# An attention and mixture-of-experts kernel: elementwise work on shared weights and on the residual moved between GpSimd and VectorE

## The chip, the core and the metric

The kernel runs on one core of a Trainium2 chip. The core has five engines that run their own instruction streams and meet at semaphores: TensorE (PE, matrix products; PEld is its weight load), VectorE (DVE), ScalarE (ACT), GpSimd (POOL) and SyncE (SP, which here only issues DMAs). The metric is the device time of one execution in microseconds (us). The kernel before takes 664.94 us, the median of 6 runs that lie between 659.42 and 669.69 us.

## The reference

Four sequences of 512 tokens with 256 features go through two residual blocks.

```python
# block 1: an expert chosen per sequence, then attention with 16 heads that share one key and value
expert = argmax(cond_8, -1)
hidden = silu(x @ W_up[expert].T + b_up) * (x @ W_gate[expert].T + b_gate)
c = hidden @ W_down[expert].T + b_down
q = (c @ Wq.T + bq) / 4 ;  k, v = split(c @ Wkv.T + bkv)
x = x + softmax(q @ k.T) @ v @ Wo.T + bo
# block 2: a linear map mixed per sequence, then a routed feed-forward net, 2 of 8 experts
masked_w = weight * mask[None]                     # weight is [8, 256, 256]
w_bot = einsum('bg,got->bot', cond_8, masked_w)    # one mixed 256x256 weight per sequence
z = x @ w_bot.T + bias
x = x + ffn(z)                                     # router, capacity 128, gelu, combine
```

Three elementwise parts of this matter here: `weight * mask` (8 tiles of 128x512 numbers), the sum over the 8 masked weights for each sequence (8 multiply-adds of 128x512 per sequence), and the addition of `bo` to the residual `x` of each sequence (4 tiles of 128x256).

## The kernel before, in words

**Phases.** The first expert net and the projections of sequence 0 run alone (up to about 43 us). Then comes one long loop over steps n = -8 to 64, of 4 quarters i each, that does the attention of all four sequences (to about 388 us); its gaps are filled with the other matrix work. Then 18 routed units of the feed-forward net run one after the other on PE (to about 606 us), and a tail writes the last rows.

**A step.** The loop stands at lines 1370 to 1393. In each quarter it issues `maxima` for the step 8 ahead (one matmul at L444 into one of 3 buffers `pm`, then a DVE maximum at L446), `exponentials` (a matmul at L473 into one of 2 buffers `pe`, then an ACT exponential at L474), whatever is pending, and then, in the third quarter of every even step, `weigh` (L483: 16 matmuls of two finished steps with the values). Such a quarter is said to weigh; it issues no further matrix work. After that come the pieces that were put at this step and quarter with `at(n, i, ...)`. In the other quarters `pump` takes pieces of side work from `tracks`, each a list of pieces with a start step and an end step, the one furthest behind first. From step 38 on, a quarter in `shut` issues a `fill` in place of `pump`: one matmul on zeros (L499).

**Engine order.** Each engine works through its instructions in exactly the order of these calls. An instruction that waits holds back everything behind it on its engine, and nothing else.

**The parts that the change touches.** The masks are multiplied on GpSimd while the loads of `w2` are issued (L249 to L252). `mixing(b, g)` (L567) adds one masked weight to the mixed weight `wb`; for sequences 0 and 1 it is two GpSimd instructions (L582, L583; L579 for g = 0), for 2 and 3 one DVE instruction (L577; L575 for g = 0). `residual(b)` (L558) loads `x` into one buffer, `residual_bias(b, n)` (L563) adds `bo` to a quarter of it on GpSimd. `prepared` (L585) is three DVE instructions at step -5: a copy of a 0/1 pattern, `spread`, and two products that make `bias2_b`, which `router_bias` (L592) reads one step later. `routed_weights(b)` (L598) turns `wb` on PE (L606) and multiplies it with the router's weight (L619); it comes after the last `mixing` of its sequence. `finish(b)` (L632) uses `x` in its first four pieces (L650) and `wb` in `mix` (L691). The scatter of finished rows (L839) and the loads of the first routed weights (L1082, L1108) are issued from GpSimd's queue.

Of the kernel before, what the change touches and what calls it, by code (L numbers as in the profile page):

```python
# [9 lines left out]
F32 = mybir.dt.float32  # L10
# [4 lines left out]
ALU = mybir.AluOpType  # L15
# [3 lines left out]
P = 128  # L19
# [3 lines left out]
D = 256  # L23
NE = 8
# [30 lines left out]
def adaln_attn_ffn_kernel(  # L55
# [21 lines left out]
    nc = tc.nc  # L77
# [24 lines left out]
    def side():  # L102
        while len(pending) > (0 if opened or crossed else 1):
            take_out()
        crossed[:] = opened
        return pside.tile([P, 512], F32, tag="side", name="side")
# [39 lines left out]
    seqs = [{} for _ in range(B)]  # L146
# [16 lines left out]
    def load(ap, shape, name):  # L163
        t = const.tile(shape, F32, name=name)
        nc.sync.dma_start(t, ap)
        return t
# [8 lines left out]
    bo_sb = load(bo[0:1, :].to_broadcast([P, D]), [P, D], "bo_sb")  # L175
    bias_x = const.tile([P, DX], F32, name="bias_x")
    nc.sync.dma_start(bias_x[:, 0:D], bias2[0:1, :].to_broadcast([P, D]))
    bias2c_sb = load(bias2c, [P, 2], "bias2c_sb")
# [4 lines left out]
    ones = const.tile([P, P], F32, name="ones")  # L183
# [34 lines left out]
    spread = const.tile([P, P], F32R, name="spread")  # L218
    bias2_b = const.tile([P, 2, P], F32, name="bias2_b")
# [11 lines left out]
    for n in range(2):  # L231
        t = const.tile([P, P], F32, name=f"negm{n}")
        nc.gpsimd.memset(t, 0.0)
        negm.append(t)
    for n in range(B):
        t = const.tile([P, 4, 32], F32, name=f"v{n}")
# [3 lines left out]
    rp = ctx.enter_context(tc.tile_pool(name="rp", bufs=1))  # L240
    attn_ctx = ExitStack()
    apool = attn_ctx.enter_context(tc.tile_pool(name="apool", bufs=1))
    for n in range(4):
        t = apool.tile([P, 4, T], F32R, name=f"qq{n}")
        nc.gpsimd.memset(t[64:65].bitcast(F32), 0.0)
        qq.append(t)
    w2_sb = apool.tile([P, NE, 2 * D], F32, name="w2_sb")
    m2_sb = cp.tile([P, 2 * D], F32, name="m2_sb", bufs=1)
    nc.sync.dma_start(m2_sb, mask2.rearrange("p c o -> p (c o)"))  # L249
    for g in range(NE):  # L250
        nc.sync.dma_start(w2_sb[:, g, :], w2[:, g].rearrange("p c o -> p (c o)"))
        nc.gpsimd.tensor_tensor(w2_sb[:, g, :], w2_sb[:, g, :], m2_sb, ALU.mult)  # L252
    bqs_sb = const.tile([P, 2], F32, name="bqs_sb")

    qp = attn_ctx.enter_context(tc.tile_pool(name="qp", bufs=1))
    ep = attn_ctx.enter_context(tc.tile_pool(name="ep", bufs=2))
# [304 lines left out]
        seqs[b]["x"] = t  # L561

    def residual_bias(b, n):  # L563
        t = seqs[b]["x"][:, n, :]
        nc.gpsimd.tensor_tensor(t, t, bo_sb, ALU.add)  # L565

    def mixing(b, g):  # L567
        if g == 0:
            seqs[b]["wb"] = rp.tile([P, 2, DX], F32, name="wb", bufs=2)
        wb = seqs[b]["wb"][:, :, 0:D]  # L570
        w = w2_sb[:, g, :].rearrange("p (c o) -> p c o", c=2)
        k = cond_sb[:, b * NE + g : b * NE + g + 1]
        if b > 1:
            if g == 0:
                nc.vector.tensor_scalar(wb, w, k, None, ALU.mult)  # L575
            else:
                nc.vector.scalar_tensor_tensor(wb, w, k, wb, ALU.mult, ALU.add)  # L577
        elif g == 0:
            nc.gpsimd.tensor_scalar(wb, w, k, None, ALU.mult)  # L579
        else:  # L580
            t = rp.tile([P, 2, D], F32, name="wk")
            nc.gpsimd.tensor_scalar(t, w, k, None, ALU.mult)  # L582
            nc.gpsimd.tensor_tensor(wb, wb, t, ALU.add)  # L583

    def prepared():  # L585
        nc.vector.tensor_copy(spread, bias2_b[:, 0])
        for c in range(2):
            nc.vector.tensor_scalar(
                bias2_b[:, c, :], ones, bias2c_sb[:, c : c + 1], None, ALU.mult
            )  # L590

    def router_bias():  # L592
        pl = pex.tile([P, T], F32, name="pe")
        for c in range(2):
            mm(pl[:, 0:NE], bias2_b[:, c, :], wr_sb[:, c, :], start=c == 0, stop=c == 1)
        return lambda: nc.scalar.copy(bias_x[:, D:DX], pl[:, 0:NE])

    def routed_weights(b):  # L598

        s = seqs[b]  # L600

        def turned():
            pt = side()
            for oc in range(2):
                for c in range(2):
                    nc.tensor.transpose(  # L606
                        pt[:, ds(oc * D + c * P, P)], s["wb"][:, c, ts(oc, P)], ident
                    )

            def take():  # L610
                s["wbT"] = rp.tile([P, 2, D], F32, name="wbT")
                nc.scalar.copy(s["wbT"].rearrange("p o c -> p (o c)"), pt)
            return take

        def times():
            pl = side()
            for c in range(2):
                for oc in range(2):
                    mm(  # L619
                        pl[:, ts(c, NE)], s["wbT"][:, oc, ts(c, P)], wr_sb[:, oc, :],  # L620
                        start=oc == 0, stop=oc == 1,
                    )

            def take():
                nc.scalar.copy(
                    s["wb"][:, :, D:DX], pl[:, 0 : 2 * NE].rearrange("p (c e) -> p c e", c=2)
                )
            return take

        return [(512, turned), (512, times)]  # L630
# [639 lines left out]
    def defer(take):  # L1270
        if take and take is not OPEN:
            pending.append(take)

    def track(start, end, pieces):
        tracks.append([start, end, sum(c for c, _ in pieces), 0, list(pieces)])
# [33 lines left out]
    track(18, 32, conditioned(3))  # L1309
    track(32, 35, project(3))  # L1310
    for b in range(B):
        track(*((11, 16), (27, 32), (50, 54), (60, 64))[b], routed_weights(b))
    rest = [finish(b) for b in range(B - 1)]
    for b in range(B - 1):
        track(16 * b + 22.75, 16 * b + (28, 28, 24.5)[b], rest[b][:4])
# [6 lines left out]
    def at(n, i, what, *args):  # L1322
        later.setdefault((n, i), []).append((what, args))
# [16 lines left out]
            sides.add((end + 5, 2))  # L1340
    for b in range(B):
        at((14, 30, 45, 58)[b], 0, residual, b)
        for n in range(4):
            at((17, 33, 46, 61)[b] + n // 2, 2 * (n % 2), residual_bias, b, n)
        for g in range(NE):
            n, i = divmod((0, 64, 167, 223)[b] + (4, 4, 4, 2)[b] * g, 4)
            at(n, i, mixing, b, g)
            shut.add((n, i))
    for i in range(9):
        at(4 + 2 * i, 0, clear, i)  # L1350
    units = [("first", n) for n in range(FIRST)] + [("early", n) for n in range(EARLY)]
# [2 lines left out]
        ("last", 1), ("last", 5), ("last", 2), ("last", 3),  # L1354
    ]
    ahead, turned, go, _ = routed(units[:-1])
    at(-5, 0, prepared)
    at(-4, 1, lambda: defer(router_bias()))
    first = list_parts(full_list("first", FIRST))
    for k in range(12):  # L1360
# [170 lines left out]
```

## Time and profile before

One execution was profiled. It took 665.37 us, and its span, first to last instruction, is 663.7 us.

| | busy us | share of the span | instructions |
|---|---|---|---|
| PE | 622.6 | 94% | 2812 |
| DVE | 342.7 | 52% | 916 |
| ACT | 238.0 | 36% | 430 |
| POOL | 173.2 | 26% | 179 |

A busy share is a mean over phases with different limits, and the records of matmuls overlap, so that PE can show as busy and still wait a little. In a table by stretches, a row has the stretch in us from the span's start, its length, the busy time and number of instructions of each engine, then the granted TensorE clock (1.00 is full speed), and what the DMA engines did. In a timeline, a row has the start, the duration, the engine, the line, the operation, the tiles and the number of instructions merged into the row; in square brackets stand the idle time of the engine before it and what ended it. In a row of a group of instructions, "busy, mean" is followed by the engine's idle time just before them.

### The profile page before, as it was taken

How to read it: one execution, taken by the hardware profiler on the slowest of the kernel's cores; microseconds unless marked ns; L12 is line 12 of the kernel's file. 1: busy time of each engine (PE TensorE's matmuls, PEld its weight loads, DVE VectorE, ACT ScalarE, POOL GpSimd, SP SyncE). 2: the span in 40 equal slices, each digit the busy share in tenths (PEclk: the TensorE clock that was granted, in tenths of full speed). 3: DMA queues.
4: the chain of work that ended last, by engine and by line, in shares of the span. 5: the costliest groups of instructions: out<-in, count | busy, mean ns of one | idle time of the engine just before them, and what ended most of it. 6: DMA issues, size and time to landing. Idle time of an engine off the chain costs nothing.

```text
span 663.7 us, 8215 instructions
## 1 busy us (share of the span) xinstructions
PE 622.6 (94%) x2812; PEld 408.4 (62%) x2812; DVE 342.7 (52%) x916; ACT 238.0 (36%) x430; POOL 173.2 (26%) x179
## 2 busy tenths in 40 slices
PE   8989999999999999899997879999999999999992
PEld 3444454454465555555454357888888897878882
DVE  3379866668766568888685441256212221223231
ACT  2231556565555455555454541211211112111110
POOL 7496000049000100042032250106312222021331
PEclk9999999999999999999797898999999999999997
DMA  7673275558321242333023836536765778456221
GB/s 240 225 180 129 91 224 157 173 152 258 114 65 38 82 129 55 97 89 112 24 92 97 315 114 262 156 121 212 227 172 160 236 230 250 149 162 193 61 26 17
DMA packets 53844, 97.64 MB, mean 147 GB/s; under 512 B 8418, under 2 KB 37378, under 8 KB 49154
## 3 DMA queue, kind: packets, MB, share of 16 engines
q1 hardware_dynamic: 46562, 81.98, 38.6%
q0 software_dynamic: 7232, 15.04, 9.6%
q8 instruction: 25, 0.41, 0.2%
q14 instruction: 25, 0.20, 0.1%
HBM read 67.50 MB, written 29.50 MB: 146 GB/s over the span
## 4 chain that ended last, share of the span: by engine, by line
PE 69%; DMA 12%; DVE 6%; POOL 5%; ACT 3%; issue 2%; SPq 1%; another core or an unknown queue 1%; POOLq 0%; DVEq 0%
PE psC L1216 14%; PE psA L1150 12%; PE pa L483 9%; PE pe L473 8%; PE pm L444 8%; DMA out_dram<-y,at 7%; PE side L338 4%; PE side L322 3%; DVE negm L446 2%; PE side L691 2%; PE side L369 2%; PE side L643 2%; ACT e L474 2%; POOL w_sb L252 2%; DMA inv_rows<-invs 2%
## 5 line engine op out<-in xcount | busy, mean ns | idle before, releaser
L446 DVE TENSOR_REDUCE negm<-pm 128x1 f32<-128x512 f32 x256 | 168.0, 684 | 61.7 <-PE pm L444 58.7
L474 ACT ACTIVATE e<-pe 128x512 f32<-128x512 f32 x256 | 148.2, 599 | 137.5 <-PE pe L473 125.6
L444 PE MATMUL pm<-kk,qq 65*128 65x512 f32 x256 | 146.8, 579 | 4.0 <-DVE negm L446 2.5
L1216 PE MATMUL psC<-wo_sb,hT 128*128 128x256 f32 (+2 forms) x544 | 115.2, 381 | 1.0 <-DVE xTr L1127 1.0
L473 PE MATMUL pe<-qq,kk 67*128 67x512 f32 x256 | 109.1, 431 | 6.9 <-ACT e L474 6.4
L1150 PE MATMUL psA<-xTr,wi_sb 128*128 128x256 f32 (+5 forms) x512 | 109.4, 371 | 3.4 <-ACT hT L1154 3.4
L1216 PEld LDWEIGHTS psC<-wo_sb,hT 128*128 128x128 f32 (+2 forms) x544 | 93.2, 182 | 17.2 <-issue 1.7
L1154 ACT ACTIVATE hT<-psA 128x512 f32<-128x512 f32 (+3 forms) x72 | 38.9, 544 | 180.7 <-PE psA L1150 162.5
L1150 PEld LDWEIGHTS psA<-xTr,wi_sb 128*128 128x128 f32 x512 | 92.2, 194 | 17.9 <-ACT hT L1154 3.6
L1196 POOL DMA_INDIRECT out_dram<-y,at x34 | 52.3, 1538 | 186.1 <-DVE w L1176 78.4
L444 PEld LDWEIGHTS pm<-kk,qq 65*128 65x128 f32 x256 | 49.1, 192 | 60.0 <-issue 24.7
L473 PEld LDWEIGHTS pe<-qq,kk 67*128 67x128 f32 x256 | 50.0, 196 | 40.5 <-ACT e L474 28.0
L338 PE MATMUL side<-xT_sb,w 128*128 128x512 f32 x128 | 62.4, 596 | 4.7 <-ACT u L295 2.6
L483 PE MATMUL pa<-e,v 128*32 128x512 f32 x512 | 66.2, 637 | 0.0
L1127 DVE COPY xTr<-psC 128x512 f32<-128x512 f32 (+5 forms) x18 | 10.5, 594 | 82.6 <-PE psC L1123 77.1
L1193 DVE TENSOR_SCALAR y<-psC,w 128x256 f32<-128x256 f32 (+1 forms) x30 | 14.4, 481 | 74.4 <-PE psC L1216 74.4
L565 POOL TENSOR_TENSOR x<-x,bo_sb 128x256 f32<-128x256 f32 x16 | 12.3, 785 | 137.4 <-DMA x<-in_xtok_dram 81.9
L839 POOL DMA_INDIRECT xp<-x,to_i x32 | 32.2, 1007 | 48.4 <-DVE negm L446 27.5
L338 PEld LDWEIGHTS side<-xT_sb,w 128*128 128x128 f32 x128 | 23.7, 190 | 22.0 <-issue 10.3
L483 PEld LDWEIGHTS pa<-e,v 128*32 128x32 f32 x512 | 13.8, 112 | 32.3 <-issue 32.0
L322 PE MATMUL side<-hid,w 128*128 128x512 f32 x64 | 31.6, 595 | 0.4 <-DVE hid L304 0.3
L582 POOL TENSOR_SCALAR wk<-w_sb,cond_sb 128x512 f32<-128x512 f32 x14 | 22.6, 1612 | 1.0
(274 smaller groups left out, 536.8 us busy)
## 6 DMA issues: line engine op xcount, KB each, us to landing
wi_sb<-in_wi_dram SPq DMA_DIRECT2D x14, 1024.0 KB
wo_sb<-in_wo_dram SPq DMA_DIRECT2D x14, 1024.0 KB
xp<-zeros SPq DMA_DIRECT2D x8, 1072.0 KB
qq<-qd SPq DMA_DIRECT2D x32, 256.0 KB
ov<-o SPq DMA_DIRECT2D x16, 256.0 KB
xt<-xp SPq DMA_DIRECT2D x15, 268.0 KB
w<-in_wcond_dram SPq DMA_DIRECT2D x12, 256.0 KB
wi_sb<-in_wi_dram POOLq DMA_DIRECT2D x3, 1024.0 KB
```

The source lines that it names most:

```text
L322: mm(po, wd[:, hc, ts(dc, P)], s["hid"][:, hc, :], start=hc == 0, stop=hc == 3)
L338: mm(s["ps"], s["w"][:, ds(first + P * c, P)], s["xT"][:, c, :], start=c == 0, stop=c == 1,)
L444: mm(pm, qq[u % 4][0:KMAX, hh, ts(i, P)], kk[0:KMAX, :], start=True, stop=True)
L446: nc.vector.tensor_reduce(negm[u % 2][:, c : c + 1], pm, AX.X, ALU.max, negate=True)
L473: mm(pe, kk[0:KEXP, ts(kc, P)], qq[u % 4][0:KEXP, i, :], start=True, stop=True)
L474: nc.scalar.activation(e_of[n][:, i, :], pe, AF.Exp)
L483: mm(pa_of[u][32 * i : 32 * i + 32, :], seqs[u // 4]["v"][:, kc, :], e[:, i], start=False, stop=kc == 3,)
L839: i = nc.gpsimd.indirect_dma_start(out=xp, out_offset=bass.IndirectOffsetOnAxis(ap=to_i[:, k, ch : ch + 1], axis=0), in_=s["x3"][:, ch, :] ...
L1150: mm(ph[:, f, :], wi_of[t][:, c, ts(first + f, P)], xT_of[t][:, c, 0:size], start=c == 0, stop=c == 1,)
L1154: nc.scalar.activation(hT_of[t][:, ds(first, per), 0:size], ph, AF.Gelu_apprx_tanh)
L1196: a = nc.gpsimd.indirect_dma_start(out=out_rows, out_offset=bass.IndirectOffsetOnAxis(ap=at[0:m, i : i + 1], axis=0), in_=y[0:m, i, :], in ...
L1216: mm(po[lo : lo + m, i % 2, :], hT_of[t][:, fc, ds(i * P, m)], wo_of[t][:, fc, :], start=fc == lo // REST, stop=fc >= F // P - (2 if m <= ...
```

## The change

- The 8 mask products go from GpSimd, at the load, to DVE (`masked`), at the third quarter of steps 0, 2, ..., 14. All but the first of these quarters weigh.
- The mixed weights of sequences 0 and 1 go from GpSimd to DVE, in the form that sequences 2 and 3 already had (2 GpSimd instructions become 1 DVE instruction). Sequence 0's stand at the second quarter of the odd steps 3 to 17, sequence 1's at quarters that weigh, steps 18 to 32.
- Sequence 2's mixed weights, on DVE as before, are spread from steps 41 to 48 (one a step) over steps 40 to 51 (one every 6 quarters). Two of the eight stand at quarters that weigh.
- The residual's bias goes from GpSimd (16 instructions of 128x256) to DVE (8 of 128x512), up to 6 steps later than before.
- `prepared` goes from DVE at step -5 to GpSimd, into the set-up part, ahead of the loop.
- The tracks of `routed_weights` for sequences 0, 1 and 2 move to later steps.

```diff
     for g in range(NE):
         nc.sync.dma_start(w2_sb[:, g, :], w2[:, g].rearrange("p c o -> p (c o)"))
-        nc.gpsimd.tensor_tensor(w2_sb[:, g, :], w2_sb[:, g, :], m2_sb, ALU.mult)
     bqs_sb = const.tile([P, 2], F32, name="bqs_sb")
+    nc.gpsimd.tensor_copy(spread, bias2_b[:, 0])
+    for c in range(2):
+        nc.gpsimd.tensor_scalar(
+            bias2_b[:, c, :], ones, bias2c_sb[:, c : c + 1], None, ALU.mult
+        )
...
     def residual_bias(b, n):
-        t = seqs[b]["x"][:, n, :]
-        nc.gpsimd.tensor_tensor(t, t, bo_sb, ALU.add)
+        t = seqs[b]["x"][:, ds(2 * n, 2), :]
+        nc.vector.tensor_tensor(t, t, bo_sb.unsqueeze(1).to_broadcast([P, 2, D]), ALU.add)
+
+    def masked(g):
+        nc.vector.tensor_tensor(w2_sb[:, g, :], w2_sb[:, g, :], m2_sb, ALU.mult)
...
         k = cond_sb[:, b * NE + g : b * NE + g + 1]
-        if b > 1:
-            if g == 0:
-                nc.vector.tensor_scalar(wb, w, k, None, ALU.mult)
-            else:
-                nc.vector.scalar_tensor_tensor(wb, w, k, wb, ALU.mult, ALU.add)
-        elif g == 0:
-            nc.gpsimd.tensor_scalar(wb, w, k, None, ALU.mult)
+        if g == 0:
+            nc.vector.tensor_scalar(wb, w, k, None, ALU.mult)
         else:
-            t = rp.tile([P, 2, D], F32, name="wk")
-            nc.gpsimd.tensor_scalar(t, w, k, None, ALU.mult)
-            nc.gpsimd.tensor_tensor(wb, wb, t, ALU.add)
-
-    def prepared():
-        nc.vector.tensor_copy(spread, bias2_b[:, 0])
-        for c in range(2):
-            nc.vector.tensor_scalar(
-                bias2_b[:, c, :], ones, bias2c_sb[:, c : c + 1], None, ALU.mult
-            )
+            nc.vector.scalar_tensor_tensor(wb, w, k, wb, ALU.mult, ALU.add)
...
-        track(*((11, 16), (27, 32), (50, 54), (60, 64))[b], routed_weights(b))
+        track(*((20, 26), (37, 42), (51.5, 54.5), (60, 64))[b], routed_weights(b))
...
     for b in range(B):
         at((14, 30, 45, 58)[b], 0, residual, b)
-        for n in range(4):
-            at((17, 33, 46, 61)[b] + n // 2, 2 * (n % 2), residual_bias, b, n)
+        for n in range(2):
+            at((19, 35, 51, 61)[b] + (2, 2, 2, 1)[b] * n, 1, residual_bias, b, n)
         for g in range(NE):
-            n, i = divmod((0, 64, 167, 223)[b] + (4, 4, 4, 2)[b] * g, 4)
+            n, i = divmod((13, 74, 162, 223)[b] + (8, 8, 6, 2)[b] * g, 4)
             at(n, i, mixing, b, g)
             shut.add((n, i))
+    for g in range(NE):
+        at(2 * g, 2, masked, g)
...
-    at(-5, 0, prepared)
```

## The prediction

> **What bounds the kernel now.** I read the busy time by stretches first, since the share over the span mixes phases.
>
> ```profile
> core 0: us, PE busy (x) PEld busy (x) DVE busy (x) ACT busy (x) POOL busy (x), PEclk, DMA share, GB/s
> 44.00:72.00 28.00, 26.48 (x80) 14.16 (x79) 26.13 (x45) 5.34 (x9) 16.83 (x12) 1.00 0.50 137
> 72.00:158.00 86.00, 83.50 (x366) 43.82 (x365) 60.61 (x105) 50.89 (x93) 16.15 (x13) 1.00 0.59 177
> 158.00:250.00 92.00, 89.41 (x399) 48.05 (x398) 61.28 (x106) 50.17 (x92) 10.82 (x11) 0.98 0.34 97
> 250.00:315.00 65.00, 61.82 (x311) 34.41 (x310) 55.70 (x134) 36.95 (x68) 11.67 (x14) 1.00 0.30 90
> 315.00:388.00 73.00, 66.50 (x309) 33.97 (x308) 46.62 (x159) 35.88 (x67) 15.79 (x21) 0.84 0.35 123
> ```
>
> PE binds the loop. DVE is its rival only at two places: before step 0 (44 to 72 us: 93% busy) and from 250 to 315 us (86%). From 72 to 250 us, where most of the new DVE work goes, it is 67 to 70% busy. After 388 us nothing is changed. The waits say the same: from 72 to 158 us DVE's maxima wait 18.6 us for PE, and PE waits 0.3 us for DVE.
>
> Next, the timelines, for what GpSimd's work does to DVE:
>
> ```profile
> 25.04 10.70 POOL L252 TENSOR_TENSOR w_sb<-w_sb,m_sb 128x512 f32<-128x512 f32 x8 [11.40 <-DMA w_sb<-in_w_dram]
> ...
> 31.58 1.63 DVE L395 TENSOR_TENSOR qL<-q,qH 128x512 fp32r<-128x512 f32 x1
> 34.05 0.57 DVE L381 CAST qH<-q 128x512 fp32r<-128x512 f32 x1 [0.84 <-ACT q L377]
> 34.66 1.64 DVE L395 TENSOR_TENSOR qL<-q,qH 128x512 fp32r<-128x512 f32 x1
> ...
> 39.44 3.70 PE L338 MATMUL side<-xT_sb,w 128*128 128x512 f32 x8 [0.63 <-ACT u L295]
> 43.34 0.47 PE L444 MATMUL pm<-kk,qq 65*128 65x512 f32 x1 [0.20 <-DMA qq<-qd]
> ```
>
> L395 takes 1.63 us beside the masks and 0.68 us with GpSimd idle (its shortest of 8 is 681 ns). The maxima, which read PSUM, show no such thing: 665 to 694 ns throughout.
>
> ```profile
> 55.38 0.50 DVE L586 CAST spread<-bias_b 128x128 fp32r<-128x128 f32 x1
> ...
> 55.91 1.51 DVE L588 TENSOR_SCALAR bias_b<-ones,bias2c_sb 128x128 f32<-128x128 f32 x2
> ...
> 58.13 0.47 PE L444 MATMUL pm<-kk,qq 65*128 65x512 f32 x1 [1.25 <-POOL wb L583]
> ```
>
> PE's 1.25 us are put down to GpSimd, but L444 doesn't read `wb`. The maxima behind L588 start at 57.35, and PE goes on when the first has emptied a `pm` buffer: the wait is `prepared`'s. The chain of waits names GpSimd before 57 us for the same false reason; I don't count it.
>
> Last, a quarter that weighs, where DVE idles while PE does 1.85 us of L483:
>
> ```profile
> 112.42 1.29 DVE L446 TENSOR_REDUCE negm<-pm 128x1 f32<-128x512 f32 x2 [1.66 <-PE pm L444]
> ```
>
> **The change part by part**, on the profiled execution (665.37 us, 0.43 above the median of the runs).
>
> *Start, -1.1 us.* Without masks on GpSimd each L395 is 0.95 us shorter. The second query waits for the first L395 (ACT idles 2.24 us), so the second L395 ends 2.1 us sooner, and the queries' DMAs and L313 with it. PE takes of this the 0.63 us that it waited for `u` (whose L291 waited 2.44 us for L313), 0.26 us inside the 3.70 (8 such matmuls at 0.43 us are 3.44) and the 0.20 us for `qq`: 1.1 us. Between 0 and -2.1.
>
> *`prepared`, -1.25 us.* DVE loses 0.50 + 1.51 us where it is 93% busy; PE gets its wait back. On GpSimd the three stand after the `qq` memsets (end 13.6 us), need `bias2c` (issued at 16.6 us), and are used at step -4 (59.5 us). Between 0 and -2.0.
>
> *GpSimd's mixing of sequence 1, -0.8 us.* From 142 to 166 us it stretches DVE's L395 (1.18 and 0.94 for 0.68), L381 (0.69 for 0.43), L409 (0.71 for 0.41) and L527 (1.22 for 0.19): 2.35 us. Little reaches PE: L418 waits 0.79 us for `kv`, behind the queries. I take that; between 0 and -2.4.
>
> *Masks, 0.* Nearest row: L395 alone, the same operation and shape, 0.68 us; eight are 5.4 us. Seven stand in quarters that weigh, under 1.66 us of DVE idling. If that cover is gone, 0.68 each: 0 to +5.4. The weights were loaded by 36 us, 36 us before the first mask.
>
> *Sequence 0's mixing, +0.7 us.* 0.48 (L575) + 7 x 0.743 (L577) = 5.7 us at quarters that do not weigh. The same instructions from 250 to 315 us hold 2.2% of that stretch's chain of waits, 1.4 us of their 5.7: 25%, with DVE 86% busy. In 72 to 158 us DVE goes from 60.6 to some 71.7 us, 83%, coming from 70%; I take half of that quarter, 12%. Between 0 and +5.7. Behind each stands the next maximum, and PE can run ahead by three `pm` buffers.
>
> *Sequence 1's mixing, 0.* Another 5.7 us, all in quarters that weigh, one per two steps; at 25% +1.4.
>
> *Residual's bias, +0.8 us.* Eight of 0.68 us (as L395) replace 12.3 us on GpSimd. Two are at steps 35 and 37, where DVE is 84% busy: 25%, 0.35. Six at 12%: 0.5. Between 0 and +5.4. They wait for `x`: if it came late all maxima would queue behind. GpSimd began its adds at 141.3, 221.8, 302.0 and 364.4 us, so `x` was there; the new places (L473 of steps 19, 35, 51, 61) start at 163.8, 249.4, 322.4 and 371.7: 7 us of margin at least.
>
> *Sequence 2's mixing, -0.3 us.* The same eight instructions; two now stand in quarters that weigh: 2 x 0.74 x 25% = 0.4, less a little for the late ones. Between -1.4 and +0.3.
>
> *Moved tracks and GpSimd's queue, 0.* The same PE work per sequence moves inside a loop that PE binds. GpSimd loses 10.7 + 3.8 + 22.6 + 19.3 + 12.3 = 68.7 us, but its scatters wait for DVE's row numbers. No DMA is moved past another on SP.
>
> Sum: -1.1 - 1.25 - 0.8 + 0.7 + 0.8 - 0.3 = -1.95, so 663.4 for an execution like the profiled one, 663.0 as a median.
>
> [...] The granted clock first:
>
> ```profile
> 226.10:229.50 3.40, 3.40 (x19) 2.50 (x18) 2.43 (x4) 2.65 (x6) 0.00 (x0) 1.00 0.00 0
> 229.50:232.90 3.40, 3.40 (x6) 1.68 (x6) 1.44 (x3) 1.40 (x3) 0.00 (x0) 0.50 0.03 5
> ```
>
> PE shows no idle stretch, and yet the next 3.4 us run at half speed: short delays can cost the clock. [...]
>
> Against moving work to DVE: L839, GpSimd's scatter, takes 1.25 us at 346.8 us beside a DVE L577, and 0.97 at its shortest. [...] The scatters run at 289 to 300, 340 to 351 and after 385 us, where hardly any DVE work is new.
>
> **Rivals.** (1) *DVE becomes the bound in steps 3 to 37*: `pm` backs up behind the mixing and the bias, which then cost full length. Against it: 18.6 us of DVE waiting for PE; for it: DVE at 83%, and PE's weight loads for L444 already wait 21.8 us for maxima over the whole run. Gains stay at -3.45; 5.7 + 5.4 = 11.1 on top give 673.0, 672.6 as a median. It decides once PE waits over 5 us for DVE from 72 to 250 us. (2) *GpSimd's contention was worth its full length*: lower bounds -2.1 - 2.0 - 2.4 - 1.4 = -7.9 with nothing paid: 657.5, 657.0 as a median. For it: DVE and PE are both full from 44 to 72 us, so each us saved may count on both. Against it: PE's own waits there are 1.5 us. (3) *The clock*: two more 6.8 us windows at half speed, +6.8 at most, 669.8; two fewer, 656.2. (4) *The change doesn't do what it says*: sequence 0's mixing stands in no quarter that weighs; that is in the sum.
>
> **How the numbers follow.** Forecast 0.57, rival 1 0.14, rival 2 0.19, rival 3 0.10 split evenly. The single runs before spread by 10 us, and a change of under 1% (6.6 us) is about what can't be told from none. Rival 2, half of rival 3 and a forecast that misses low give 0.25 below 658.3; rival 1, the other half and one that misses high give 0.18 above 671.6; 0.57 between. The range, 655 to 673, reaches to rival 2 with a shorter clock loss below and to rival 1 above; some 2 in 10 lie outside.
>
> **What would show it.** Right: L395 at 0.7 us near 32 us, first L444 near 42.2 us, no 1.25 us wait near 57 us, DVE near 78 to 83% from 72 to 158 us with PE still waiting under 2 us for it, L527 at 0.2 us throughout. Wrong: `negm` on the chain of waits from 72 to 250 us beyond 5%, a DVE wait for `x`, or half-speed windows before 229 us.

## The result and the profile after

The changed kernel takes 669.78 us (median; 664.44 to 676.53), the kernel before 665.47 us in all its runs beside it. The ratio is 1.0074, 95% interval 1.0058 to 1.009: the change makes the kernel slower by about 4.9 us by this ratio (by 4.3 us between the two medians). The forecast was 663.0 us, 1.95 us less than before: the sign is wrong, though the time lies inside the wide range. Ratios, and the half-speed times below, leave out the runs that took over 1.5% longer than the fastest of their kernel. The profiled execution took 669.92 us, its span is 668.2 us, its mean granted clock 0.969, as before.

The busy time by the same stretches, after:

```profile
core 0: us, PE busy (x) PEld busy (x) DVE busy (x) ACT busy (x) POOL busy (x), PEclk, DMA share, GB/s
44.00:72.00 28.00, 27.73 (x87) 15.46 (x85) 25.92 (x44) 7.42 (x13) 0.00 (x0) 1.00 0.49 143
72.00:158.00 86.00, 82.99 (x365) 42.14 (x364) 69.17 (x122) 50.22 (x92) 0.00 (x0) 1.00 0.62 180
158.00:250.00 92.00, 88.11 (x396) 48.32 (x396) 67.22 (x119) 51.13 (x93) 0.00 (x0) 1.00 0.30 89
250.00:315.00 65.00, 61.33 (x308) 33.59 (x307) 51.62 (x125) 34.60 (x66) 8.66 (x10) 0.97 0.29 86
315.00:388.00 73.00, 65.43 (x296) 31.52 (x299) 45.79 (x153) 34.85 (x66) 10.74 (x16) 0.84 0.36 123
```

GpSimd is empty from 44 to 250 us, and DVE is 80% busy from 72 to 158 us, as forecast. The last two rows hold fewer instructions of PE and DVE than before: work is late there. The same engines' timelines at the start (DVE, then PE) show the gain:

```profile
31.54 0.69 DVE L399 TENSOR_TENSOR qL<-q,qH 128x512 fp32r<-128x512 f32 x1
33.06 0.43 DVE L385 CAST qH<-q 128x512 fp32r<-128x512 f32 x1 [0.84 <-ACT q L381]
33.53 0.69 DVE L399 TENSOR_TENSOR qL<-q,qH 128x512 fp32r<-128x512 f32 x1
...
56.66 1.37 DVE L450 TENSOR_REDUCE negm<-pm 128x1 f32<-128x512 f32 x2 [0.40 <-PE pm L448]
```

```profile
41.67 0.68 PE L448 MATMUL pm<-kk,qq 65*128 65x512 f32 x1
```

L399 (L395 before) takes 0.69 us in place of 1.63, the first maximum's matmul starts at 41.67 in place of 43.34 us, and without `prepared` between the maxima near 57 us PE's wait of 1.25 us is gone. How this gain is kept and lost is read by comparing the start of the same step (its first `pe` matmul, L473 before, L477 after) in the two traces:

| step | 0 | 14 | 16 | 36 | 42 | 46 | 50 | 54 | 56 | 58 | 62 |
|---|---|---|---|---|---|---|---|---|---|---|---|
| before, us | 71.8 | 137.6 | 147.9 | 252.5 | 278.4 | 296.9 | 314.5 | 335.3 | 344.3 | 359.6 | 374.7 |
| after less before, us | -3.1 | -3.0 | -3.9 | -4.7 | -1.3 | +1.0 | -0.2 | +4.7 | +8.1 | +3.6 | +3.6 |

The changed kernel is 4.7 us ahead at step 36. It loses this and more at steps 36 to 46 and 50 to 56. (The 4.5 us that it regains between 56 and 58 are a pause in the trace of before: ACT idles 4.7 us near 350 us, and no record says for what. Such a pause of 4.7 to 5.2 us, with 3.4 or 6.8 us at half speed behind it, is in five of the twelve traces of kernels whose second half of sequence 2's router stands at its old place, and in none of the eight where it is moved. One trace of a kernel can't tell how often its runs have it.)

What happens near step 53 shows the kind of loss. PE's timeline before, and after:

```profile
333.15 0.20 PE L782 MATMUL side<-hot,upto_b 128*128 128x64 bf16 x1
333.19 0.19 PE L786 MATMUL side<-prev,ones_b 128*128 128x64 bf16 x1
333.22 0.17 PE L790 MATMUL side<-total,ones_b 128*128 128x16 bf16 x1
333.25 0.47 PE L444 MATMUL pm<-kk,qq 65*128 65x512 f32 x1
333.79 0.50 PE L473 MATMUL pe<-qq,kk 67*128 67x512 f32 x1
334.13 0.40 PE L543 MATMUL side<-inv_rows,spread 128*128 128x512 f32 x1
```

```profile
334.55 0.17 PE L783 MATMUL side<-total,ones_b 128*128 128x16 bf16 x1
335.32 1.03 PE L612 MATMUL side<-wr_sb,wbT 128*128 128x8 f32 x8 [0.60 <-DVE m L459]
336.20 0.47 PE L448 MATMUL pm<-kk,qq 65*128 65x512 f32 x1
336.52 0.39 PE L477 MATMUL pe<-qq,kk 67*128 67x512 f32 x1
337.66 0.79 PE L547 MATMUL side<-inv_rows,spread 128*128 128x512 f32 x1 [0.75 <-ACT wb L618]
```

The second half of sequence 2's router (L612; L619 before) was done at step 52.0 before. Now it stands between the counts (L775 to L783) and L547, and all of them take turns in the `side` banks. PE waits 0.60 us for DVE, does 1.03 us of matmuls with only 8 columns, and waits 0.75 us for ACT's copy. By stretches of 3.4 us, after:

```profile
333.70:337.10 3.40, 2.60 (x17) 1.76 (x16) 2.76 (x7) 1.98 (x5) 0.00 (x0) 1.00 0.23 82
337.10:340.50 3.40, 2.84 (x8) 1.62 (x8) 2.31 (x10) 1.10 (x3) 0.00 (x0) 0.50 0.01 5
340.50:343.90 3.40, 3.40 (x11) 1.50 (x14) 2.97 (x10) 1.79 (x3) 0.00 (x0) 0.50 0.02 5
343.90:347.30 3.40, 3.40 (x17) 0.90 (x10) 0.00 (x0) 0.00 (x0) 2.75 (x3) 0.50 0.23 81
```

Waits of 1.35 us in all, none longer than 0.75, are followed by 10.2 us at half the granted clock (1.00, then 0.50 three times). Other such waits are new: 2.0 us at step 42.25 (L779, whose input L764 stands on DVE behind the output's add L643, a mixing L583 and a maximum; 0.8 us before), 1.1 us at step 20.25 (L342 for DVE's `hid`; 1.0 us of it also in early_mix1 below, which is faster than the kernel before), 1.5 us at step 51.5 (L599 for the last mixing).

These waits cost time by themselves, beside what the clock costs. The two profiled executions have the same mean clock and yet differ by 4.55 us. From the start of step 0 to that of step 54 the changed kernel takes 7.7 us more; in that stretch PE idles 14.5 us after and 8.9 us before, and 16.5 and 13.7 us run at half speed. So in this pair of traces about 5.6 us are direct waiting and about 1.4 us the clock.

### The profile page after: what moved, and what is told of

It reads as the page before. It is cut to its first block, busy times and chain, and to the rows that moved or that the text cites. A ratio compares the mean times of both kernels' runs of the same rounds, so it can differ in the third digit from the quotient of the medians.

```text
span 668.2 us, 8192 instructions
## 1 busy us (share of the span) xinstructions
PE 623.5 (93%) x2812; PEld 406.6 (61%) x2812; DVE 352.9 (53%) x945; ACT 237.5 (36%) x430; POOL 105.7 (16%) x128
## 4 chain that ended last, share of the span: by engine, by line
PE 75%; DMA 10%; DVE 8%; ACT 3%; issue 2%; SPq 1%; POOLq 0%; another core or an unknown queue 0%; DVEq 0%
PE psC L1209 14%; PE psA L1143 12%; PE pa L487 10%; PE pm L448 9%; PE pe L477 8%; PE side L342 7%; DMA out_dram<-y,at 7%; PE side L326 4%; DVE negm L450 3%; PE side L373 3%; PE side L684 2%; PE side L636 2%; ACT e L478 2%; DMA inv_rows<-invs 2%; PE pa L503 1%
## 5 line engine op out<-in xcount | busy, mean ns | idle before, releaser
L448 PE MATMUL pm<-kk,qq 65*128 65x512 f32 x256 | 148.4, 585 | 2.7 <-DVE negm L450 2.3
L477 PE MATMUL pe<-qq,kk 67*128 67x512 f32 x256 | 107.9, 426 | 3.5 <-ACT e L478 2.5
L1143 PE MATMUL psA<-xTr,wi_sb 128*128 128x256 f32 (+5 forms) x512 | 106.7, 365 | 3.4 <-ACT hT L1147 3.4
L1143 PEld LDWEIGHTS psA<-xTr,wi_sb 128*128 128x128 f32 x512 | 90.3, 190 | 17.1 <-ACT hT L1147 3.6
L477 PEld LDWEIGHTS pe<-qq,kk 67*128 67x128 f32 x256 | 50.1, 196 | 35.5 <-ACT e L478 23.2
L487 PE MATMUL pa<-e,v 128*32 128x512 f32 x512 | 68.8, 660 | 0.0
L342 PE MATMUL side<-xT_sb,w 128*128 128x512 f32 x128 | 62.3, 597 | 4.2 <-ACT u L299 1.9
L1120 DVE COPY xTr<-psC 128x512 f32<-128x512 f32 (+5 forms) x18 | 10.5, 594 | 81.6 <-PE psC L1116 77.7
L751 POOL COPY x<-top 128x8 f32<-128x8 f32 x4 | 1.4, 350 | 282.6 <-DVE top L728 282.6
L342 PEld LDWEIGHTS side<-xT_sb,w 128*128 128x128 f32 x128 | 23.6, 190 | 22.0 <-issue 9.4
L487 PEld LDWEIGHTS pa<-e,v 128*32 128x32 f32 x512 | 14.2, 115 | 33.5 <-issue 33.1
L300 DVE SCALAR_TENSOR_TENSOR u<-th,u 128x512 f32<-128x512 f32 x16 | 11.1, 691 | 19.1 <-ACT u L299 19.1
```

Of the source, the lines that this page charges most:

```text
L342: mm(s["ps"], s["w"][:, ds(first + P * c, P)], s["xT"][:, c, :], start=c == 0, stop=c == 1,)
L448: mm(pm, qq[u % 4][0:KMAX, hh, ts(i, P)], kk[0:KMAX, :], start=True, stop=True)
L477: mm(pe, kk[0:KEXP, ts(kc, P)], qq[u % 4][0:KEXP, i, :], start=True, stop=True)
L487: mm(pa_of[u][32 * i : 32 * i + 32, :], seqs[u // 4]["v"][:, kc, :], e[:, i], start=False, stop=kc == 3,)
L1143: mm(ph[:, f, :], wi_of[t][:, c, ts(first + f, P)], xT_of[t][:, c, 0:size], start=c == 0, stop=c == 1,)
```

## Experiments

The interval of each ratio is 95%, against the kernel before run on the same chip. "Half-speed time" is worked out for each run from its mean granted clock, which in the traces before and after is 1.00 or 0.50 at any moment, never between: (1 - clock) x 2 x span. Its median was 33.7 us over 144 runs of the kernel before (30.4 to 35.7 by chip) and 44.2 us over 38 of the changed one. Compared within each chip, a run of the kernel before is 0.45 us longer for each us at half speed (correlation 0.84); for the changed kernel it is 0.44 us. So the 10.5 us more would go with 4.6 us. That is a correlation, which the fills below test, and it leaves the direct waits out: the 4.9 us would then be the clock and the new waits together, less what the early part gains.

### Which part costs

Three theories came first: L (sequence 2's new places), B (the residual's bias on VectorE) and R (the first rival: DVE binds in steps 3 to 37). Four kernels take the change apart.

```diff
 # seq2_old: the changed kernel, sequence 2's mixing and router as before
-    track(*((20, 26), (37, 42), (51.5, 54.5), (60, 64))[b], routed_weights(b))
+    track(*((20, 26), (37, 42), (50, 54), (60, 64))[b], routed_weights(b))
-    n, i = divmod((13, 74, 162, 223)[b] + (8, 8, 6, 2)[b] * g, 4)
+    n, i = divmod((13, 74, 167, 223)[b] + (8, 8, 4, 2)[b] * g, 4)
 # bias_pool: the changed kernel, the bias on GpSimd at its old places
-    t = seqs[b]["x"][:, ds(2 * n, 2), :]
-    nc.vector.tensor_tensor(t, t, bo_sb.unsqueeze(1).to_broadcast([P, 2, D]), ALU.add)
+    t = seqs[b]["x"][:, n, :]
+    nc.gpsimd.tensor_tensor(t, t, bo_sb, ALU.add)
-    for n in range(2):
-        at((19, 35, 51, 61)[b] + (2, 2, 2, 1)[b] * n, 1, residual_bias, b, n)
+    for n in range(4):
+        at((17, 33, 46, 61)[b] + n // 2, 2 * (n % 2), residual_bias, b, n)
 # seq2_only: the kernel before with sequence 2's two lines alone changed
 # early_only: the kernel before with masks, preparations, sequence 0's mixing and router changed
 # early_mix1: both undone, that is early_only and sequence 1's mixing and router
```

> The changed kernel with sequence 2's mixed weights and router pieces put back to their old steps (41.75 to 48.75, track 50 to 54); all else as changed. Theory L (the loss comes late: sequence 2's last mixed weight at step 51 makes PE wait at step 51.5, PE then works too thinly and the clock falls to half speed in steps 50 to 56): 665 us, some 4 to 5 below the changed kernel's 669.8. Theory B (the loss is the residual's bias on VectorE): 669 to 670. Theory R (rival 1 of the prediction: the masks and mixed weights on VectorE in steps 0 to 34 cost it): 669 to 670.

> The changed kernel with the residual's bias back on GpSimd at its old steps; all else as changed. Theory B: 666 us or less, 3 to 5 below the changed kernel. Theory L: 668.5 to 669.5. Theory R: 669 to 670.

> The kernel before with only the early half of the change: masks and sequence 0's mixed weights on VectorE at the new quarters, the two preparations on GpSimd, sequence 0's router pieces at steps 20 to 26. Theories L and B: 662 to 663 us, 2 to 4 below the kernel before, the gain of the start (1.7 us at the first L444, 3.1 us at step 0 in the profiles) kept to the end. Theory R: 666 or more.

> The kernel before with only sequence 2's mixed weights and router pieces at the new steps (40.5 to 51.0, track 51.5 to 54.5). Theory L: 669 to 670 us, 4 to 5 above the kernel before, with a lower granted clock in steps 50 to 56. Theories B and R: 665 to 666.

> The changed kernel with both late parts undone: the residual's bias on GpSimd at its old places, and sequence 2's mixing and router at their old places; the masks, the two preparations and the mixings of sequences 0 and 1 stay changed. If the costs of the two late parts add, 669.8 - 2.2 - 3.6 = 664.0 us, within 1 us, and step 16 starts 3 to 4 us sooner than before the change. If the loss is in mixing sequence 1 on VectorE or in the first two routers' new places, 666 or more. Theory C (PE runs thin in some 3.4 us window and the next runs at half speed): time at half speed 34 to 38 us per run, between the kernel before (34.5) and the changed one (44.2).

> The same kernel that ran at ratio 0.9966 (0.9929 to 1.0004): masks, preparations and the mixings of sequences 0 and 1 changed, all else as before. If the early part is worth 3 to 4 us whatever the chip, 0.994 to 0.998; if that was one chip's, 0.998 to 1.002.

| kernel | ratio to before | half-speed us (before there) |
|---|---|---|
| changed | 1.0074 (1.0058 to 1.009) | 44.2 (33.7 over all chips) |
| seq2_old | 1.0036 (1.0003 to 1.007) | 38.5 (34.5) |
| bias_pool | 1.0029 (1.0001 to 1.0056) | 41.9 (34.5) |
| seq2_only | 1.0071 (1.0034 to 1.0108) | 39.4 (34.5) |
| early_only | 0.9993 (0.9965 to 1.002) | 36.4 (34.5) |
| early_mix1 | 0.9966 (0.9929 to 1.0004) | 32.8 (31.7) |
| early_mix1_again | 0.9954 (0.9917 to 0.9991) | 30.2 (30.4) |

R falls: with the masks and two mixings on DVE the kernel is faster, by 0.40% in the mean of two runs (2.7 us). On this footing the bias costs 0.76% (seq2_old against 0.996), sequence 2's places 0.69% (bias_pool), both together 1.14%. Taken out of the changed kernel, the bias is worth 0.45% and sequence 2's places 0.38%. The two costs do not quite add, but each interval is some 0.3% wide on either side. early_only came out as no theory had it: not 662 to 663 us but 664.72. In its trace 2.5 of the 2.9 us won at step 0 are gone by step 8, behind a half-speed window at 78.7 us.

### Which half of sequence 2's move

```diff
 # track2: the kernel before, router of sequence 2 alone; first half to 51.5, second to 53.25
-    track(*((11, 16), (27, 32), (50, 54), (60, 64))[b], routed_weights(b))
+    track(*((11, 16), (27, 32), (51.5, 54.5), (60, 64))[b], routed_weights(b))
 # collide: the kernel before, (50, 55.4): only the second half moves, 52.0 to 53.25
 # first_only: the kernel before, (51.5, 52.5): only the first half moves, 50.0 to 51.5
 # second_late: the changed kernel, (51.5, 56): its second half goes on to 54.0
```

> The kernel before with only the router of sequence 2 moved from steps 50 to 54 to steps 51.5 to 54.5; its mixing keeps its old places and ends at step 48.75. Theory W (the cost of sequence 2's new places is PE's direct wait for the last mixing, 1.5 us at L599's transposes): that wait is gone, time 664 to 666. Theory C: PE's work in steps 50 to 51.5 gets thinner and that after 52 thicker whatever the mixing does, and 2 us or more of the 3.4 us remain: 666.5 to 668.5, time at half speed above 37 us.

> The kernel before with one piece moved: the second half of sequence 2's router (L619, four small matmuls and a copy on ACT) from step 52.0 to step 53.25, between the counts' matmuls and L543, where the changed kernel has it; its first half and all mixing stay. Theory K (it is this meeting that costs: three uses of the side banks within 1.5 us, PE waits 0.5 us for L619 and 0.75 to 0.93 us for ACT's copy at L543, PE streams a quarter of that 3.4 us window, and the next runs at half speed): ratio 1.004 to 1.007, time at half speed 5 to 9 us above that of the kernel before, PE waits at L543 again. Rival F (the first half's move from step 50 to 51.5 costs): ratio 0.998 to 1.002.

> The kernel before with only the first half of sequence 2's router (L606, four transposes and a copy on ACT) moved from step 50.0 to 51.5; the second half stays at 52.0 and the mixing as it was. Theory K (the second half's meeting with L543 costs): 0.998 to 1.002. Rival F (the first half's move costs): 1.004 to 1.007.

> The changed kernel with only that second half (L612 there) moved on from step 53.25 to step 54.0, behind L547; the late mixing, its wait of 1.5 us at L599 and the residual's bias stay. Theory K: the wait at L547 goes, and the time falls by 2 to 4 us: ratio to the kernel before 1.001 to 1.004 in place of 1.0074. Rival F, and the theory that the wait at L599 is what costs: ratio 1.006 to 1.009.

Measured: track2 1.0068 (1.0036 to 1.01), collide 1.0028 (0.9985 to 1.0071), first_only 1.0029 (1.0 to 1.0059), second_late 1.0047 (1.0012 to 1.0081). Two pieces of PE work, moved by about a step and a half, cost as much as the whole change does; the mixing's new places add nothing that the ratios show (1.0071 with them, 1.0068 without), but the intervals allow some 3 us either way, and the trace of seq2_only has the direct waits of 2.0 us at step 42.25 (0.8 before) and 1.5 us at L606, the L599 of after. PE's timeline of track2 has the meeting at step 53.25, on a kernel that is otherwise the one before:

```profile
332.21 1.03 PE L619 MATMUL side<-wr_sb,wbT 128*128 128x8 f32 x8 [0.46 <-DVE m L455]
...
334.56 0.51 PE L543 MATMUL side<-inv_rows,spread 128*128 128x512 f32 x1 [0.75 <-ACT wb L625]
```

Theory K, that this meeting alone costs, isn't shown: the two halves come out alike, and each alone is barely told from nothing. Their sum, 0.57%, agrees with track2. collide does have the meeting in its trace (0.47 us at L619, 0.75 us at L543, and 6.8 us at half speed behind them), but over its runs the half-speed time is 36.6 us against 35.7 before, not the 5 to 9 us more that K asks for. first_only has 35.7 us against 30.4 with no wait of PE that the trace of before lacks, so what it costs, if it does, is not found. In second_late's profiled execution (674.92 us, the slowest of its 13) the wait at L547 is gone, and one of 1.2 us at L612 has come, so little is won; its gain on the changed kernel, 0.27%, is within the intervals.

### Is it the clock

If short waits cost by way of the clock, then matmuls that compute nothing, put ahead of the waits, should win time; put where PE is full, they should cost. `extra` puts k matmuls on zeros into the open `pa` bank (0.22 us each at full speed in the trace of fills).

```diff
+    def extra(n, k):
+        for _ in range(k):
+            first = not pa_of
+            if first:
+                pa_of[n // 4] = ppv.tile([P, 512], F32, name="pa")
+            mm(pa_of[max(pa_of)], zeros_b[:, 0:P], zeros_b, start=first, stop=False)
...
+            extra(n, EXTRA.get((n, i), 0))
             if busy:
                 continue
 # fills: the changed kernel
+    EXTRA = {(1, 2): 3, (2, 0): 3, (20, 1): 4, (42, 1): 4, (51, 2): 4, (51, 3): 3, (53, 1): 3, (53, 2): 3}
 # fills_full: the changed kernel, 3 each at (5, 3), (7, 1), (9, 3), (11, 1), (13, 3), (25, 3), (27, 1), (29, 3), (31, 1)
 # early_fill: early_only, {(1, 2): 4, (2, 0): 4, (20, 1): 4}
 # before_fill: the kernel before, {(2, 0): 3, (17, 3): 3, (21, 3): 4, (34, 1): 3, (42, 1): 3, (49, 3): 3, (51, 2): 3}
 # early_mix1_fill: early_mix1, 29 matmuls at nine waits
```

> The changed kernel with 27 more matmuls on zeros (0.21 us each, 5.7 us in all) put ahead of PE's eight waits of 0.7 to 2.2 us at steps 1.5, 2.0, 20.25, 42.25, 51.5, 52.0, 53.25 and 53.5. They compute nothing. Theory C: PE streams in windows that were thin, the time at half speed falls from 44 us to 36 to 40, and the time by 0.44 of that to 666 to 668.5. Theory W: PE only does something else while it waits; time 669.5 to 671, time at half speed stays above 42.

> The changed kernel with the same 27 matmuls on zeros as in the run with fills at its waits, but at nine quarters in steps 5 to 13 and 25 to 31, where PE streams over 85% of the time. Theory C: nothing is gained, the time at half speed stays at the changed kernel's (some 9 us above that of the kernel before), and PE pays up to 5.7 us: ratio 1.008 to 1.014. If any extra matmuls raise the clock: ratio 1.002 to 1.005, as with the fills at the waits (1.0037).

> The kernel with only the early part (masks and sequence 0's mixing on VectorE, preparations on GpSimd), and 12 more matmuls on zeros ahead of PE's waits at steps 1.5, 2.0 and 20.25. Theory C: no window at half speed near 78 us in most executions, the start's gain of 3 us is kept to step 16, 662 to 663.5 us, time at half speed 33 to 35. Theory W: 664.5 to 666, as without the fills.

> The kernel before with 22 matmuls on zeros (0.21 us each) ahead of seven of its waits of 0.7 to 1.3 us (steps 2.0, 17.75, 21.75, 34.25, 42.25, 50.0, 51.75). Theory C: time at half speed falls by 4 to 8 us, ratio 0.994 to 0.997, so that half or more of the 0.9918 is the early part's own. If the fills alone made that ratio: 0.991 to 0.993.

> The kernel that ran at ratio 0.9966 (masks, preparations and the mixings of sequences 0 and 1 changed; the residual's bias and sequence 2 as before), and 29 matmuls on zeros (0.21 us each) ahead of nine waits of PE of 0.7 to 1.3 us. Theory C (thin windows cost the clock): time at half speed some 5 us below that of the kernel before, ratio 0.991 to 0.996. If the fills cost as much as the clock gives: 0.996 to 0.999.

| kernel | ratio to before | half-speed us (before there) |
|---|---|---|
| fills | 1.0037 (1.0009 to 1.0064) | 28.4 (31.7) |
| fills_full | 1.0224 (1.0174 to 1.0273) | 48.5 (30.4) |
| early_fill | 0.9997 (0.9958 to 1.0035) | 30.3 (31.7) |
| before_fill | 0.9968 (0.9938 to 0.9997) | 24.9 (30.4) |
| early_mix1_fill | 0.9918 (0.9885 to 0.9951) | 25.0 (35.7) |

The same 27 matmuls win 0.37% ahead of the waits (some 0.3% on either side) and cost 1.5% where PE is full, so it isn't the number of matmuls. Ahead of the waits they take the half-speed time from some 10 us above that of the kernel before to 3 us below. Filling an idle stretch doesn't shorten it, so what they win comes, as far as the runs show, by the clock: 15.8 us less at half speed are worth 7 us at 0.44, and the matmuls take up to 5.9. At step 53.25 the program of fills still has the meeting and the wait of 0.75 us; by stretches of 3.4 us:

```profile
330.80:334.20 3.40, 2.65 (x18) 1.81 (x16) 1.94 (x7) 0.77 (x3) 0.00 (x0) 1.00 0.26 89
334.20:337.60 3.40, 3.40 (x20) 1.53 (x22) 3.08 (x9) 2.39 (x4) 0.00 (x0) 1.00 0.00 0
337.60:341.00 3.40, 3.40 (x23) 2.21 (x16) 2.62 (x8) 0.91 (x2) 1.15 (x2) 1.00 0.00 0
```

PE is as thin as it was (2.65 against 2.60 us busy), but in this execution full speed follows. PE's waits of the changed kernel at steps 42.25 and 51.5, and what is left of them with the fills ahead (PE's waits from 72 to 345 us, the longest of each; after, then fills):

```profile
PE side L779 <- DVE prev L764: 2.0, 1, 2.0
...
PE side L599 <- DVE wb L583: 1.5, 1, 1.5
```

```profile
PE side L787 <- DVE prev L772: 1.2, 1, 1.2
...
PE side L607 <- DVE wb L591: 0.6, 1, 0.6
```

fills_full cost more than its matmuls: 1.5% is 10 us, 27 x 0.22 are 5.9; its half-speed time rose too, against the forecast of theory C, and why isn't known. early_fill won clock (half-speed time from 1.9 us above to 1.4 below that of before) and no time: the expected 662 to 663.5 us did not come. The kernel before gains 0.32% from fills of its own. Of the 0.82% of early_mix1_fill about half is the early part's (0.40%) and half the fills'. That kernel beats both: 658.38 against 664.36 us on its chip.

### What makes the bias cost

```diff
 # bias01: early_mix1, the bias of sequences 0 and 1 on VectorE at the changed kernel's places
+    at((19, 35)[b] + 2 * n, 1, residual_bias, b, n)
 # bias01_weigh: the same adds in quarters that weigh
+    at(((16, 16), (34, 36))[b][n], 2, residual_bias, b, n)
 # bias23: early_mix1, the bias of sequences 2 and 3 alone on VectorE, at the changed kernel's places
```

> The kernel with masks, preparations and the mixings of sequences 0 and 1 changed and sequence 2 as before (ratio 0.9966 when it ran), and in it the residual's bias of sequences 0 and 1 alone on VectorE (steps 19, 21, 35, 37). Two earlier runs put all of the bias at 0.7%, 4.6 us, on this footing. If the cost is general (each add at full length in a busy stretch, or a clock lost at step 20), half of it comes here: ratio 0.999 to 1.002. If it is sequence 2's adds at steps 51 and 53, beside the router: ratio 0.995 to 0.998.

> The early part (0.9966 and 0.9954 in two runs) with the residual's bias of sequences 0 and 1 on VectorE, as in the run that gave 1.0028, but in quarters that weigh, where DVE idles 1.66 us: both adds of sequence 0 at step 16, those of sequence 1 at 34 and 36. If the place costs (DVE ahead of what PE waits for at steps 20.25 and 36.0): ratio 0.994 to 0.998. If the adds cost wherever they stand: 1.000 to 1.005.

> The early part with the residual's bias of sequences 2 and 3 alone on VectorE at the changed kernel's places (steps 51, 53, 61, 62); that of sequences 0 and 1 on GpSimd as before. If nearly all of the bias' cost is that of sequences 0 and 1: ratio 0.994 to 0.998. If the costs are alike: 0.999 to 1.003.

Measured: bias01 1.0028 (0.9993 to 1.0063), bias01_weigh 0.9937 (0.9898 to 0.9976), bias23 0.999 (0.996 to 1.0019). The place costs, not the add: four adds of 0.68 us move the time by 0.9% with their quarters (0.4 to 1.4% by the two intervals). bias23, 0.3% above the early part, lies between its two forecasts, and its interval reaches into both. DVE's timeline near step 20, in early_mix1 and in bias01:

```profile
162.99 0.69 DVE L300 SCALAR_TENSOR_TENSOR u<-th,u 128x512 f32<-128x512 f32 x1 [0.75 <-ACT u L299]
163.60 1.88 DVE L450 TENSOR_REDUCE negm<-pm 128x1 f32<-128x512 f32 x3
165.40 0.74 DVE L308 SCALAR_TENSOR_TENSOR hid<-side,w,u 128x512 f32<-128x512 f32 x1
```

```profile
162.94 0.69 DVE L300 SCALAR_TENSOR_TENSOR u<-th,u 128x512 f32<-128x512 f32 x1 [0.75 <-ACT u L299]
163.55 0.68 DVE L573 TENSOR_TENSOR x<-x,bo_sb 128x512 f32<-128x512 f32 x1
164.16 1.88 DVE L450 TENSOR_REDUCE negm<-pm 128x1 f32<-128x512 f32 x3
165.95 0.74 DVE L308 SCALAR_TENSOR_TENSOR hid<-side,w,u 128x512 f32<-128x512 f32 x1
```

The add (L573) stands in a queue of DVE's on which PE's L342 waits: `hid` starts 0.55 us later, and L342 with it (166.19 and 166.75 us; its own wait is 1.0 and 1.1 us, since PE has by then also waited 0.24 us for a maximum). At step 36.0, PE's timeline of bias01 has a wait that early_mix1 lacks:

```profile
248.78 0.50 PE L448 MATMUL pm<-kk,qq 65*128 65x512 f32 x1 [0.44 <-DVE negm L450]
```

These are 1.0 us of the 0.68%, 4.5 us, that bias01 lies above the two runs of early_mix1. The half-speed time (37.8 us, 2.1 above that of before; early_mix1 0.5 above in the mean) would add 0.7 us. The rest isn't found; the intervals allow 1.5 to 7.5 us. The trace of bias01 also has the pause of ACT (4.8 us, then 6.8 us at half speed), which those of early_mix1, its repeat and bias01_weigh lack; whether its runs have it more often isn't known.

## Why the prediction was wrong, point by point

**Right.** *Start, prepared, sequence 1's contention, masks and two mixings*: their terms add to -1.1 - 1.25 - 0.8 + 0 + 0.7 + 0 = -2.45 us; measured alone they give 0.40%, -2.7 us. That they agree so well is partly luck: early_only, which holds -1.65 us of them, gave -0.5 us (interval -2.3 to +1.3), which leaves some -2.2 us for sequence 1's contention and mixing, priced at -0.8. In the trace, step 0 starts 3.1 us earlier (2.35 forecast), and 0.9 us more come between steps 14 and 16, where L531 now takes 0.19 us. The cover of the masks holds: DVE is 80% busy from 72 to 158 us, and PE waits 1.2 us for it (0.3 before). No instruction of DVE waits for `x`. No half-speed window lies before 229 us in this trace; those of four kernels with the same start (early_only, seq2_old, bias_pool, second_late) have one at 78 to 79 us, and collide, with the old start, has one at 80 us.

**Rival 1** did not come about: PE waits about 3 us for DVE from 72 to 250 us (5 was the point from which it decides), though `negm` has 5.3% of the chain there, just over the 5% named, and 2.2% before.

**The steps that failed.** *"Moved tracks and GpSimd's queue, 0."* The reason given, the same PE work inside a loop that PE binds, fails in steps 50 to 54, where PE waits in turn for ACT and DVE through the `side` banks: the router's move alone measured +0.68%, 4.5 us. New waits of 1.2 us are seen in its trace (0.46 and 0.75); how the rest arises, the clock apart, is open. *"Sequence 2's mixing, -0.3 us"* left out that L599 and L779 would wait for DVE behind it: the traces show 2.7 us more waiting there, outside the term's range, though no cost shows in the ratios within some 3 us. *"Residual's bias, +0.8 us"* was mis-sized: measured 0.76%, 5 us, by the ratio of seq2_old to early_mix1 and its repeat, or 0.45%, 3 us, by the changed kernel against bias_pool. It was priced as a share (12% or 25%) of DVE's busy time; what counted was what stood behind each add. Two of the four adds of sequences 0 and 1 delay a PE that is waiting, and in quarters that weigh the four show no cost.

**The clock** was kept as a rival that could go either way, after one row had shown it falling without an idle gap. That row's "no idle stretch" rests on PE's busy time, 3.40 of 3.40 us; by the columns of its matmuls PE streamed 0.61 of the time there, by the estimate of the last section. In the trace before, the half-speed windows of the loop last 3.4 us (from 229.5 and 328.5 us) and 6.8 us (from 314.8, 352.4 and 376.3 us), all at 0.50. An estimate from that, 3.4 us lost in one of 6.8 us, is what rival 3's 6.8 us for two stands on. The half-speed time rose by some 10 us, which at 0.44 us each goes with 4.6 us. The forecast lacked a sign there, and the direct waits besides: the trace after has new waits of PE of 0.6 to 2 us at four places, and each was to be had from the order of the instructions on DVE and in the `side` banks. That rival 3's 669.8 us meets the measured time is luck: it had two more windows as the whole price, where the runs show waits and clock less the early part's gain.

## What to carry to other kernels

Price an instruction on an in-order engine by who waits behind it at that place, not by the engine's mean load (an add of 0.68 us put `hid` and PE's L342 behind it some 0.55 us later in bias01): the same four adds showed no cost beside a block of 1.85 us matmuls, and came out 0.9% dearer where two of them stand ahead of a queue that PE waits for. A move that adds no work can have a price too: here two small pieces of PE work cost 0.68%, of which waits among users of the same few banks (0.46 and 0.75 us) are a part. Count the added short waits of PE twice, as time and as a risk to the clock, and try fills that compute nothing ahead of them: here 1.35 us of waits stood ahead of 10.2 us at a clock of 0.50, and 27 fills ahead of the waits go with a half-speed time of 28.4 us in place of 44.2.

## What the hardware showed that was not expected

In the trace after, the granted clock fell to 0.50 five times before 388 us, and the longest idle time of PE in the loop is 2.0 us. The 3.4 us ahead of each drop before 388 us held PE streaming 0.36 to 0.62 of the time, an estimate from the columns of the matmuls at the 0.23 us at which `pm` and `pe` matmuls of 512 columns follow each other at full speed (333.79, 334.02, 334.24 us), four of L487, which start together, counted as one. Drops there last 3.4, 6.8 or 10.2 us. A thin stretch stands ahead of every drop, but doesn't always bring one: by the same working no drop of the loop, in all 20 traces, follows 3.4 us with a share above 0.63, while some 20 to 28 such stretches of the trace after (by where they are cut) lie below 0.60 and bring none, and the rows of fills show another. Kernels with the same start meet drops at different places: the first is at 268.8 us in the trace after, and one stands at 78 to 79 us in those of early_only, seq2_old, bias_pool and second_late. With 27 matmuls ahead of the waits the half-speed time is 28.4 us in place of 44.2 (the kernel before: 33.7, and 31.7 beside fills).
